# Sixteen-head cross attention: scores with context tokens on partitions, maximum and sum by GpSimd, two heads at a time

## Chip, cores, metric

The program runs on one core of a Trainium2 chip. The core has five engines that run their own queues of instructions and wait for each other by semaphores: TensorE (PE in the profile; its weight loads are PEld), VectorE (DVE), ScalarE (ACT), GpSimd (POOL) and SyncE (SP), which issues the DMAs here. The metric is device time in microseconds (us), the median of several runs. All data is float32.

## What is computed

The reference passes `x` of shape (8 batches, 112 tokens, 512 channels) through four layers, with a context of shape (8, 375, 512). Layer 0 is a plain cross attention, layers 1 and 2 are recurrent token-mixing blocks, and layer 3, which matters here, is a normalization and a cross attention with 16 heads of 128, done twice with different weights, and then a perceptron with one hidden layer:

```python
def _cross_attention(q_in, kv_in, wq, bq, wk, bk, wv, bv, wo, bo, bias_k, bias_v):
    b, q_len, _ = q_in.shape
    t = kv_in.shape[1]
    qh = (q_in @ wq + bq).reshape(b, q_len, H, K)
    kh = (kv_in @ wk + bk).reshape(b, t, H, K)
    vh = (kv_in @ wv + bv).reshape(b, t, H, K)
    kh = jnp.concatenate([kh, jnp.broadcast_to(bias_k, (b, 1, H, K))], axis=1)
    vh = jnp.concatenate([vh, jnp.broadcast_to(bias_v, (b, 1, H, K))], axis=1)
    scale = jnp.sqrt(jnp.asarray(K, q_in.dtype))
    logits = jnp.einsum('bqhk,bthk->bhqt', qh, kh) / scale
    weights = jax.nn.softmax(logits, axis=-1)
    ctx = jnp.einsum('bhqt,bthk->bqhk', weights, vh).reshape(b, q_len, H * K)
    return ctx @ wo + bo
...
x = res + _cross_attention(h, xf_1, ...)
...
x = res + _cross_attention(h, xf_2, ...)
h = _layer_norm(x, ln_mlp_scale, ln_mlp_offset)
h = jax.nn.gelu(h @ w_fc1 + b_fc1, approximate=False) @ w_fc2 + b_fc2
return x + h
```

Each query has 376 scores: 375 context tokens and one learned key, `bias_k`, with the learned value `bias_v`.

## The kernel before

Activations lie with channels on partitions: `x`, `h_in`, `q`, `ctxt` are tiles of 128 partitions with the 896 tokens (8 batches of 112) along the free dimension, one block of 512 channels being four such slices.

**Attention.** `attention(i, ...)` (L1267) runs for i = 1 and 2. Its outer loop goes over 4 groups of 4 heads (`NG`, `HG`), its inner one over 8 batches: 64 batch steps in both attentions. Per group there is a query projection (`queries`, L1357), an output projection (`project7` with `w_o`), and for every second batch the keys of two batches (`key_pieces`, L1277, which runs `chained`, L1206, or, for a few, loads keys made earlier). These products are done by a scheme with seven half-size products in place of eight, for which GpSimd makes sums of weight quarters (`weight_sums`, L1122, lines 1135 to 1138: `ws..`, `wsk`). The values of all batches were computed earlier, beside layers 1 and 2, and lie in memory; each step loads its own (L1398, L1399: tile `v`, one buffer).

**One batch step** (L1393 to L1425) for four heads: GpSimd copies the learned key into column 375 of `kt` (L1396). For each head the score product has the query as the stationary operand (128x112) and the keys as the moving one (376 columns), so that queries lie on partitions: `sc` is 112x376 in PSUM (L1403). `softmax` (L229) takes VectorE's maximum along the row (L232), ScalarE's exponential with the sum accumulated (L235), VectorE's reciprocal (L236) and scaling (L237). TensorE transposes the probabilities in three pieces, tokens to partitions (L1406, `pt`); two copies by VectorE and one by ScalarE bring them to SBUF (L1410, L1412, `pts`). Then 12 products over 125, 125 and 126 tokens give `av` (L1416), and VectorE adds the bias `bv` into `ctxt` (L1423).

**Records.** A float32 product is shown as two matmul records in the trace, a transpose as one.

**PSUM** has eight banks; in layer 3 there are three for `pt`, two for `sc`, one for `av` and two for the projections and keys (`ps`, pool `t3p`).

**Order.** Layer 0 is scheduled by hand; in layer 3 the tile framework's scheduler sets each engine's order from the order in which the code issues instructions, the data they need, and the buffers that are free, so that key products of later batches stand between the steps of the softmax. The same framework puts a load of a GpSimd library into GpSimd's queue wherever an instruction follows whose code the library loaded before does not have. In the program before the change one such load stands in that queue, ahead of the first use.

After the attentions comes the perceptron (`mlp`, L1453). With the last group of the second attention (`ends`) the output projection is done in halves, after batches 4 and 7, and the normalization for the perceptron follows each.

Of the kernel before, what the change touches and what calls it, by code (L numbers as in the profile page):

```python
# [24 lines left out]
ALU = mybir.AluOpType  # L25
# [18 lines left out]
T = S + 1  # L44
CT = S // 3
# [63 lines left out]
def tile_kernel(ctx: ExitStack, tc: tile.TileContext, d: dict, out: bass.AP):  # L109
# [27 lines left out]
    ones_t, mean_h, less_mean_h = (const.tile([P, P], F32, name=f) for f in ("ones_t", "mean_h", "less_mean_h"))  # L137
    pick = const.tile([P, 4, 4 * HB], F32, name="pick")
# [983 lines left out]
    def weight_sums(pool, tag, w, u):  # L1122


        if tag == "kt":
            y = [pool.tile([P, HG, T], F32, tag=tag, name=f"ws{j}{u}", bufs=4) for j in range(2)]
# [140 lines left out]
    def attention(i, ident, h_in, work, kv, ps, ps2, keep, near, mlp_norm):  # L1267
# [9 lines left out]
        def key_pieces(gr, b, w, kts):  # L1277
# [3 lines left out]
            if ("wk", i, gr, b) in shared:  # L1281
                for j in range(2):
                    kts.append(kv.tile([P, HG, T], F32, tag="kt", name=f"k{u}_{j}", bufs=4))
# [13 lines left out]
            kt = [kv.tile([P, HG, T], F32, tag="kt", name=f"k{u}_{j}", bufs=4) for j in range(2)]  # L1297
# [58 lines left out]
        nc.vector.tensor_copy(bv, p)  # L1356
        def queries(gr):  # L1357
# [17 lines left out]

        q, pieces = queries(0)
        for gr in range(NG):
            ends = i == 2 and gr == NG - 1
            w_o = weight(f"{pre}wo{i}", gr)
# [4 lines left out]
            for b in range(B):  # L1384
                u = f"{i}_{gr}_{b}"
                tok = slice(b * L, (b + 1) * L)
                if b % 2 == 0:
                    if gr and not b:
                        w_ks.append(key_weight(gr))
# [6 lines left out]
                nc.gpsimd.tensor_copy(kt[:, :, S], over[:, gr * HG : (gr + 1) * HG])  # L1396
# [3 lines left out]
                pt = [ps2.tile([CT + 1, HG, L], F32, tag="pt", name=f"pt{u}_{t}", bufs=3) for t in range(3)]  # L1400
                for o in range(HG):
                    sc = ps2.tile([L, T], F32, tag="sc", name=f"sc{u}_{o}", bufs=2)
                    nc.tensor.matmul(sc, q[:, o, tok], kt[:, o, :], start=True, stop=True)  # L1403
                    prob = softmax(work, sc, T, f"{u}_{o}")
                    for t, (t0, nt) in enumerate(CHUNKS):
                        nc.tensor.transpose(pt[t][:nt, o, :], prob[:, t0 : t0 + nt], ident[:L, :L])  # L1406
                pts = work.tile([CT + 1, 3, HG, L], F32, tag="pts", name=f"pts{u}", bufs=1)
                for t, (_, nt) in enumerate(CHUNKS):
                    if t == 1:
                        nc.scalar.copy(pts[:nt, t], pt[t][:nt])  # L1410
                    else:
                        nc.vector.tensor_copy(pts[:nt, t], pt[t][:nt])  # L1412
                av = ps2.tile([P, HG, L], F32, tag="av", name=f"av{u}")
                for o in range(HG):
                    for t, (_, nt) in enumerate(CHUNKS):
                        nc.tensor.matmul(  # L1416
                            av[:, o, :],
# [206 lines left out]
```

## Time and profile before

| | |
|---|---|
| median of three runs | 2947.22 us (2944.2 to 2949.86) |
| span of the profiled execution | 2938.3 us |
| layers 0 to 2, values, first keys and queries | 0 to 1472 us |
| first attention's steps | 1472 to 2045 us |
| between the attentions | 2045 to 2127 us |
| second attention's steps | 2127 to 2742 us |
| last output projection and perceptron | 2742 to 2938 us |
| mean granted TensorE clock | 0.996 |

The stretches are read from the timeline, by the starts and ends of score and value products. GpSimd's own costs in the attentions are small: 64 copies of the learned key (223 ns each) and weight sums of 1.3 to 1.5 us each. The profile's rows give a source line, an engine, an operation, the tiles written and read, a count, then the busy time and the mean of one, then the idle time of the engine ahead of it with what ended it.

### The profile page before, as it was taken

To read this page: it belongs to the slowest core of one execution; us is meant where nothing else is said; L and a number is where in the kernel's file an instruction comes from. 1 tells how busy PE (TensorE), PEld (TensorE's weight loads), DVE (VectorE), ACT (ScalarE), POOL (GpSimd) and SP (SyncE) were. 2 spreads that over 40 slices of the span, in tenths; PEclk is the share of its full clock that TensorE was granted. 3 is DMA by queue.
4 is the path that set the end of the run, shared out by engine and by line. 5 is a ranking of instruction groups with operands and counts; after the bars stand their busy time and mean duration, and the time that the engine had idled before them with its cause. 6 is when DMAs were issued, how large, how long until landed. Compare 5 with 4: busy or idle time off the path is not lost.

```text
span 2938.3 us, 29915 instructions
## 1 busy us (share of the span) xinstructions
PE 2848.3 (97%) x10130; PEld 1555.3 (53%) x10130; DVE 1605.4 (55%) x2408; ACT 1020.6 (35%) x2028; POOL 870.8 (30%) x700
## 2 busy tenths in 40 slices
PE   8989999999999999999899999999999999999999
PEld 4734443344444433356465656566565656656544
DVE  1464288845442788652555555545554554545455
ACT  2232456533243565532331313232331323323311
POOL 1432178744331687641412010100302010000030
PEclk9999999999999999999999999999999999999999
DMA  5721498843311989642243334334332433432110
GB/s 208 231 76 39 156 278 258 265 128 110 99 64 62 281 234 298 184 132 90 101 149 126 124 123 129 109 122 140 102 123 100 133 108 122 139 113 80 47 51 25
DMA packets 198743, 400.82 MB, mean 136 GB/s; under 512 B 33224, under 2 KB 119528, under 8 KB 191808
## 3 DMA queue, kind: packets, MB, share of 16 engines
q1 hardware_dynamic: 198592, 398.91, 43.2%
q8 instruction: 81, 1.33, 0.2%
q14 instruction: 70, 0.57, 0.1%
HBM read 321.06 MB, written 77.91 MB: 136 GB/s over the span
## 4 chain that ended last, share of the span: by engine, by line
PE 83%; DVE 9%; ACT 3%; POOL 3%; issue 2%; DMA 1%; DVEq 0%; POOLq 0%; ACTq 0%; SPq 0%
PE ps_vk L1001 13%; PE ps_k1k L1234 10%; PE ps_k5k L1234 7%; PE av L1416 6%; PE sc L1403 5%; PE ps_o L163 3%; PE pt L1406 3%; PE ps_fk L163 2%; PE ps_k1q L1161 2%; PE ps_r L569 2%; PE ps_k L569 2%; PE ps_k5q L1161 2%; PE ps_fr L163 2%; PE ps_v L569 2%; PE ps_k7q L1161 2%
## 5 line engine op out<-in xcount | busy, mean ns | idle before, releaser
L1001 PE MATMUL ps_vk<-wv,cv 128*128 128x512 f32 x1296 | 581.7, 599 | 13.8 <-ACT k L1099 6.1
L1001 PEld LDWEIGHTS ps_vk<-wv,cv 128*128 128x128 f32 x1296 | 242.8, 191 | 337.3 <-issue 285.0
L1027 POOL TENSOR_TENSOR k<-k,k 128x512 f32<-128x512 f32 (+1 forms) x153 | 197.2, 1289 | 323.4 <-ACT k L1026 276.0
L776 DVE TENSOR_TENSOR_SCAN st<-decay,kv 128x904 f32<-128x904 f32 x128 | 260.7, 2037 | 17.5 <-POOL rs L780 4.8
L780 POOL TENSOR_TENSOR rs<-st,r 128x896 f32<-128x896 f32 x128 | 246.8, 1928 | 51.9 <-DVE st L776 46.8
L235 ACT ACTIVATE prob<-sc,top 112x376 f32<-112x376 f32 x256 | 147.2, 575 | 296.3 <-DVE top L232 168.0
L1396 POOL COPY k<-over_k 128x4 f32<-128x4 f32 x64 | 13.8, 223 | 648.6 <-PE sc L1403 576.6
L1403 PE MATMUL sc<-k,q 128*112 128x376 f32 x512 | 201.2, 485 | 1.6 <-ACT prob L235 1.5
L1416 PEld LDWEIGHTS av<-pts,v 125*128 125x128 f32 (+1 forms) x1536 | 183.4, 191 | 31.0 <-DVE pts L1412 15.8
L1416 PE MATMUL av<-pts,v 125*128 125x112 f32 (+1 forms) x1536 | 187.7, 276 | 1.9 <-DVE pts L1412 0.9
L1234 PE MATMUL ps_k1k<-cs,wsk 128*128 128x375 f32 x480 | 177.8, 478 | 4.6 <-ACT u2k L1237 3.1
L772 DVE TENSOR_TENSOR kv<-vp,k 128x904 f32<-128x904 f32 x128 | 141.5, 1105 | 58.2 <-ACT vp L674 52.4
L232 DVE TENSOR_REDUCE top<-sc 112x1 f32<-112x376 f32 x256 | 139.0, 544 | 53.7 <-PE sc L1403 49.0
L1026 ACT COPY k<-ps_vk 128x512 f32<-128x512 f32 (+1 forms) x153 | 89.1, 582 | 177.0 <-PE ps_vk L1001 174.2
L1099 ACT COPY k<-ps_vk 128x512 f32<-128x512 f32 (+1 forms) x153 | 89.0, 582 | 172.3 <-PE ps_vk L1001 164.2
L1406 PEld LDWEIGHTS pt<-ident_l,prob 112*125 112x125 f32 (+1 forms) x768 | 97.3, 175 | 72.2 <-DVE prob L237 44.8
L1406 PE MATMUL pt<-ident_l,prob 112*125 112x112 f32 (+1 forms) x768 | 120.7, 276 | 2.7 <-DVE prob L237 2.5
L1234 PEld LDWEIGHTS ps_k1k<-cs,wsk 128*128 128x128 f32 x480 | 88.7, 188 | 62.8 <-ACT u2k L1237 4.3
L237 DVE TENSOR_SCALAR prob<-prob,total 112x376 f32<-112x376 f32 x256 | 113.4, 443 | 7.7
L1241 DVE TENSOR_TENSOR k<-ps_k5k,u2k 128x375 f32<-128x375 f32 x52 | 28.5, 549 | 162.2 <-PE ps_k5k L1234 161.2
L674 ACT COPY vp<-vj 128x896 f32<-128x896 f32 x124 | 112.8, 910 | 7.3 <-DMA vj<-rows 3.5
L1423 DVE TENSOR_TENSOR ctxt<-av,bv 128x448 f32<-128x448 f32 x64 | 40.0, 625 | 128.9 <-PE av L1416 128.9
(394 smaller groups left out, 4837.0 us busy)
## 6 DMA issues: line engine op xcount, KB each, us to landing
vj<-rows SPq DMA_DIRECT2D x124, 448.0 KB
cv<-blocks SPq DMA_DIRECT2D x181, 251.5 KB
cs<-blocks SPq DMA_DIRECT2D x120, 375.0 KB
wvs<-k SPq DMA_DIRECT2D x128, 256.0 KB
v<-wvs SPq DMA_DIRECT2D x64, 512.0 KB
cx<-in_ctxT SPq DMA_DIRECT2D x38, 750.0 KB
v<-wvs SPq DMA_DIRECT2D x64, 252.0 KB
wvs<-k SPq DMA_DIRECT2D x64, 224.0 KB
```

What stands on the lines that cost most here:

```text
L163: nc.tensor.matmul(p, w[:, k, o * P : (o + 1) * P], rhs(k, h), start=k == 0, stop=k == NC - 1)
L235: nc.scalar.activation(prob, scores, AF.Exp, bias=top, accum_out=total)
L569: nc.tensor.matmul(y, ws[f][:, c, o * P : (o + 1) * P], x_f, start=c == 0, stop=c == NC - 1)
L776: nc.vector.tensor_tensor_scan(flat(st), flat(decay[:, c]), flat(kv), 0.0, ALU.mult, ALU.add)
L780: nc.gpsimd.tensor_mul(by_batch(rs), st[:, :, :L], by_batch(r[:, c, :]))
L1001: nc.tensor.matmul(to, left, right, start=start and n == 0, stop=k == 1, skip_group_check=True)
L1027: nc.gpsimd.tensor_add(y, z, y)
L1161: nc.tensor.matmul(to, lhsT, rhs, start=start and k == 0, stop=k == 1, skip_group_check=not start)
L1234: nc.tensor.matmul(y, lhsT, rhs, start=start and k == 0, stop=k == 1, skip_group_check=True)
L1403: nc.tensor.matmul(sc, q[:, o, tok], kt[:, o, :], start=True, stop=True)
L1406: nc.tensor.transpose(pt[t][:nt, o, :], prob[:, t0 : t0 + nt], ident[:L, :L])
L1416: nc.tensor.matmul(av[:, o, :], v[:nt, t, o * HD : (o + 1) * HD], pts[:nt, t, o, :], start=t == 0, stop=t == 2,)
```

## The change

The score product is turned round: a block of 128 key columns is the stationary operand, the 112 queries of a head the moving one, so that tokens lie on partitions and no transpose is needed. Three blocks start at tokens 0, 125 and 250; each is 128 wide, so that it runs over its own 125 or 126 tokens, and the key tile gets two more columns (`TK`), filled with the learned key. The surplus partitions are taken out by a bias of -1e30 in the exponential (`rests`). The maximum over tokens is then a maximum of three blocks, by VectorE, and one over partitions, by GpSimd's `partition_all_reduce`; the sum likewise, by two GpSimd adds and a second all-reduce. The division is moved behind the value product, with the bias added by ScalarE. All of it is done for two heads at a time, twice in a batch step. PSUM in layer 3 is now four banks for `sc` (two buffers of two banks), one for `av` and three for the projections and keys. The key weight of a group is asked for ahead of the output weight, and four constant tiles of the earlier layers are freed ahead of layer 3.

```diff
+TK = T + 2
...
+    marks = ExitStack()
+    marked = marks.enter_context(tc.tile_pool(name="marks", bufs=1))
+    ones_t, mean_h, less_mean_h = (marked.tile([P, P], F32, name=f) for f in ("ones_t", "mean_h", "less_mean_h"))
+    pick = marked.tile([P, 4, 4 * HB], F32, name="pick")
...
-    ones_t, mean_h, less_mean_h = (const.tile([P, P], F32, name=f) for f in ("ones_t", "mean_h", "less_mean_h"))
-    pick = const.tile([P, 4, 4 * HB], F32, name="pick")
...
-    def softmax(work, scores, n, name):
-
-        top = work.tile([L, 1], F32, tag="top", name=f"top_{name}")
-        nc.vector.tensor_reduce(top, scores, AX.X, ALU.max, negate=True)
-        prob = work.tile([L, n], F32, tag="prob", name=f"prob_{name}")
-        total = work.tile([L, 1], F32, tag="total", name=f"total_{name}")
-        nc.scalar.activation(prob, scores, AF.Exp, bias=top, accum_out=total)
-        nc.vector.reciprocal(total, total)
-        nc.vector.tensor_scalar(prob, prob, total, None, ALU.mult)
-        return prob
...
+        rests = keep.tile([P, 2], F32, tag="rests", name=f"rests{i}")
+        for y, n in enumerate((CT, CT + 1)):
+            nc.vector.tensor_reduce(rests[:, y : y + 1], ident[:, n:], AX.X, ALU.add)
+        nc.vector.tensor_scalar(rests, rests, -1e30, None, ALU.mult)
...
+        def attend(u, gr, heads, q, kt, v, ctxt, tok):
+
+            n = len(heads) * L
+            sc = ps2.tile([P, 4, 256], F32, tag="sc", name=f"sc{u}", bufs=2)
+            for t in range(3):
+                for y, o in enumerate(heads):
+                    nc.tensor.matmul(
+                        sc[:, t, y * L : (y + 1) * L], kt[:, o, t * CT : t * CT + P], q[:, o, tok], start=True, stop=True
+                    )
+            top, tops, each = (work.tile([P, n], F32, tag="top", name=f"{f}{u}", bufs=6) for f in ("top", "tops", "each"))
+            nc.scalar.copy(top, sc[:, 0, :n])
+            for t in (1, 2):
+                nc.vector.tensor_max(top, sc[:, t, :n], top)
+            nc.gpsimd.partition_all_reduce(tops, top, P, ReduceOp.max)
+            pts = work.tile([P, 3, n], F32, tag="pts", name=f"pts{u}", bufs=2)
+            nc.vector.tensor_sub(pts, sc[:, :3, :n], tops.unsqueeze(1).to_broadcast([P, 3, n]))
+            for t, y in ((slice(2), 0), (slice(2, 3), 1)):
+                nc.scalar.activation(pts[:, t], pts[:, t], AF.Exp, bias=rests[:, y : y + 1])
+            nc.gpsimd.tensor_add(tops, pts[:, 0], pts[:, 1])
+            nc.gpsimd.tensor_add(tops, pts[:, 2], tops)
+            nc.gpsimd.partition_all_reduce(each, tops, P, ReduceOp.add)
+            nc.vector.reciprocal(each, each)
+            av = ps2.tile([P, len(heads), L], F32, tag="av", name=f"av{u}")
+            for y, o in enumerate(heads):
+                for t, (_, nt) in enumerate(CHUNKS):
+                    nc.tensor.matmul(
+                        av[:, y],
+                        v[:nt, t, o * HD : (o + 1) * HD],
+                        pts[:nt, t, y * L : (y + 1) * L],
+                        start=t == 0,
+                        stop=t == 2,
+                    )
+            where = ctxt[:, heads[0] : heads[-1] + 1, tok]
+            nc.vector.tensor_mul(where, av, each.rearrange("p (o n) -> p o n", n=L))
+            for y, o in enumerate(heads):
+                nc.scalar.activation(where[:, y], where[:, y], AF.Identity, bias=column(bv, gr * HG + o))
...
+            if gr:
+                w_ks.append(key_weight(gr))
...
-                    if gr and not b:
-                        w_ks.append(key_weight(gr))
...
-                nc.gpsimd.tensor_copy(kt[:, :, S], over[:, gr * HG : (gr + 1) * HG])
+                nc.gpsimd.tensor_copy(
+                    kt[:, :, S:], over[:, gr * HG : (gr + 1) * HG].unsqueeze(2).to_broadcast([P, HG, TK - S])
+                )
                 v = kv.tile([P, 3, C], F32, tag="v", name=f"v{u}", bufs=1)
                 nc.sync.dma_start(v[:, :2], shared["wv", i, gr, b][:, :2])
                 nc.sync.dma_start(v[: CT + 1, 2], shared["wv", i, gr, b][: CT + 1, 2])
-                pt = [ps2.tile([CT + 1, HG, L], F32, tag="pt", name=f"pt{u}_{t}", bufs=3) for t in range(3)]
-                for o in range(HG):
-                    sc = ps2.tile([L, T], F32, tag="sc", name=f"sc{u}_{o}", bufs=2)
-                    nc.tensor.matmul(sc, q[:, o, tok], kt[:, o, :], start=True, stop=True)
-                    prob = softmax(work, sc, T, f"{u}_{o}")
-                    for t, (t0, nt) in enumerate(CHUNKS):
-                        nc.tensor.transpose(pt[t][:nt, o, :], prob[:, t0 : t0 + nt], ident[:L, :L])
-                pts = work.tile([CT + 1, 3, HG, L], F32, tag="pts", name=f"pts{u}", bufs=1)
-                for t, (_, nt) in enumerate(CHUNKS):
-                    if t == 1:
-                        nc.scalar.copy(pts[:nt, t], pt[t][:nt])
-                    else:
-                        nc.vector.tensor_copy(pts[:nt, t], pt[t][:nt])
-                av = ps2.tile([P, HG, L], F32, tag="av", name=f"av{u}")
-                for o in range(HG):
-                    for t, (_, nt) in enumerate(CHUNKS):
-                        nc.tensor.matmul(
-                            av[:, o, :],
-                            v[:nt, t, o * HD : (o + 1) * HD],
-                            pts[:nt, t, o, :],
-                            start=t == 0,
-                            stop=t == 2,
-                        )
-                nc.vector.tensor_add(
-                    ctxt[:, :, tok], av, bv[:, gr * HG : (gr + 1) * HG].unsqueeze(2).to_broadcast([P, HG, L])
-                )
+                for half in range(2):
+                    attend(f"{u}_{half}", gr, range(2 * half, 2 * half + 2), q, kt, v, ctxt, tok)
...
-            tc.tile_pool(name="t3p", bufs=2, space=PSUM) as ps,
+            tc.tile_pool(name="t3p", bufs=3, space=PSUM) as ps,
...
+    marks.close()
     layer3()
```

More of the change, by code (lines that the diff above doesn't have):

```diff
@@ L18 @@
 import concourse.tile as tile
+from concourse.bass_isa import ReduceOp
 from concourse import mybir
@@ L1125, in weight_sums @@
         if tag == "kt":
-            y = [pool.tile([P, HG, T], F32, tag=tag, name=f"ws{j}{u}", bufs=4) for j in range(2)]
+            y = [pool.tile([P, HG, TK], F32, tag=tag, name=f"ws{j}{u}", bufs=4) for j in range(2)]
             y = [t.rearrange("p a b -> p (a b)")[:, : 2 * C].rearrange("p (j k o) -> p j k o", j=2, k=2) for t in y]
@@ L1282, in key_pieces @@
                 for j in range(2):
-                    kts.append(kv.tile([P, HG, T], F32, tag="kt", name=f"k{u}_{j}", bufs=4))
+                    kts.append(kv.tile([P, HG, TK], F32, tag="kt", name=f"k{u}_{j}", bufs=4))
                     for t in range(3):
@@ L1296, in key_pieces @@
             nc.sync.dma_start(b22, d["ctxT"][:, b + 1, 2:])
-            kt = [kv.tile([P, HG, T], F32, tag="kt", name=f"k{u}_{j}", bufs=4) for j in range(2)]
+            kt = [kv.tile([P, HG, TK], F32, tag="kt", name=f"k{u}_{j}", bufs=4) for j in range(2)]
             kts += kt
```

## The prediction

> **What bounds the kernel now.** I read the shares of busy time first, then the chain of work that ended last.
>
> ```profile
> PE 2848.3 (97%) x10130; PEld 1555.3 (53%) x10130; DVE 1605.4 (55%) x2408; ACT 1020.6 (35%) x2028; POOL 870.8 (30%) x700
> ...
> PE 83%; DVE 9%; ACT 3%; POOL 3%; issue 2%; DMA 1%; DVEq 0%; POOLq 0%; ACTq 0%; SPq 0%
> ```
>
> TensorE is busy 97% of the span and is 83% of the chain. The change lies in one stage, so I next cut the span by stage. The columns are the stretch, its length, then busy time (instructions) of PE, PEld, DVE, ACT and POOL, the granted clock, the DMA share and GB/s.
>
> ```profile
> 1614.00:1764.00 150.00, 149.54 (x633) 94.45 (x632) 80.71 (x183) 41.96 (x108) 16.90 (x21) 1.00 0.40 127
> 2580.00:2742.00 162.00, 154.40 (x649) 97.49 (x647) 81.99 (x172) 50.28 (x120) 11.54 (x14) 1.00 0.30 95
> 2742.00:2938.00 196.00, 187.25 (x494) 92.44 (x492) 101.48 (x142) 36.92 (x55) 28.90 (x20) 1.00 0.11 37
> ```
>
> The first row is one group of four heads (eight batches): PE never stops, the clock is full, and GpSimd works 17 us of 150. The scores run from 1472 to 2742 us with one break (2045 to 2127: output projection, normalization and queries between the two attentions), so the attention loops last 573 + 615 = 1188 us, 18.6 us for each of 64 batch steps. The last row is the tail behind them, 196 us. Whatever leaves PE here is a gain, as long as no other engine needs 18.6 us a step.
>
> **What leaves PE.** The timeline of PE (start, length) gives the cadence from start to start:
>
> ```profile
> 1475.68 0.79 PE L1403 MATMUL sc<-k,q 128*112 128x376 f32 x2
> 1476.31 0.78 PE L1406 MATMUL pt<-ident_l,prob 112*125 112x112 f32 x6
> 1476.93 0.80 PE L1403 MATMUL sc<-k,q 128*112 128x376 f32 x2
> ...
> 1503.09 2.83 PE L1416 MATMUL av<-pts,v 125*128 125x112 f32 x24
> 1505.75 0.79 PE L1406 MATMUL pt<-ident_l,prob 112*125 112x112 f32 x6
> ```
>
> A step has 4 score products of 0.63 us (two records each): 2.53 us. Its 12 transposes take 0.62/6 each: 1.25 us. Its 24 value records take 2.66 us. After the change the 4 score products are 12 with 112 moving columns, 24 records of the shape of the value product: 2.66 us by that row. Saved: 2.53 + 1.25 - 2.66 = 1.12 us a step, 72 us in 64 steps. PE would then need (1188 - 72)/128 = 8.7 us for each half step of two heads, the unit in which the new code works.
>
> **What is added, and where.** The softmax of a half step now goes: ScalarE copies one score block, VectorE takes two maxima, GpSimd reduces over partitions, VectorE subtracts, ScalarE takes exponentials, GpSimd adds three blocks (two adds) and reduces again, VectorE takes reciprocals and scales, ScalarE adds the bias. For VectorE and ScalarE I have rows of the like shape; for GpSimd some.
>
> ```profile
> L706 DVE RECIPROCAL gsq<-gsq 128x224 f32<-128x224 f32 x32 | 48.2, 1523 | 24.7 <-ACT gsq L701 24.7
> L1423 DVE TENSOR_TENSOR ctxt<-av,bv 128x448 f32<-128x448 f32 x64 | 40.0, 625 | 128.9 <-PE av L1416 128.9
> L577 ACT ACT_TABLE_LOAD x14 | 18.0, 1283 | 0.2
> L858 POOL TENSOR_TENSOR x<-x,rr 128x448 f32<-128x448 f32 x16 | 18.1, 1128 | 60.1 <-DVE rr L857 60.1
> L445 POOL TENSOR_TENSOR sx<-first,xa 128x4 f32<-128x4 f32 x16 | 9.3, 584 | 0.0
> L971 POOL COPY wv<-wx 128x1024 f32<-128x1024 f32 x1 | 1.2, 1206 | 1.2 <-PE ps_vk L1001 1.2
> L1396 POOL COPY k<-over_k 128x4 f32<-128x4 f32 x64 | 13.8, 223 | 648.6 <-PE sc L1403 576.6
> ```
>
> VectorE: at 1.4 ns a column (625/448) three operations of 224 columns take 0.31 us each and the subtraction of 672 takes 0.94; with the reciprocal, 1.52, that is 3.4 us of 8.7. ScalarE's two copies, exponentials and biases are below that. Neither binds.
>
> GpSimd's queue is the question. The instruction order of the changed program shows 256 all-reduces of 128x224, 256 adds of 128x224, and also 272 instructions that nobody wrote in the diff: loads of a GpSimd library. The all-reduce stands in another library than the two-input add. Of the loads 136 lead to the all-reduce (128 before the second reduction, 8 before the maximum that opens a group) and 136 back (111 before the first add, 25 before weight sums and a key sum). In a half step the queue reads: maximum reduced, load, add, add, load, sum reduced, and then the next half's maximum with no load between. It is serial, since the adds wait for exponentials of this maximum. Behind those adds wait the sum's reduction, the next half's maximum, the `over` column of later keys (which the score product of a later batch waits for) and the weight sums.
>
> Prices. An add: between the rows of 4 and 448 columns, 224 columns take 0.58 + 0.27 = 0.85 us. The all-reduce has no row. Below, a one-input pass: between 223 ns for 4 columns and 1206 for 1024, 0.43 us. Above, folding 128 partitions in halves is seven two-input adds, 5.95 us. It must at least combine and give back, so I take two adds, 1.7 us. The Trainium skill ("GPSIMD Engine Reference", section 3.2 Cross-partition) counts partition-axis reduction among the things GpSimd is for, but its figure for a reduction along partitions of [128, 2048], 247,699 ns, would make 27 us of 224 columns; with that the sum below would be 10.7 ms, an estimate from that page.
>
> A library load has no row either. Below: 1.28 us, what ScalarE needs to load a table. Above, code that comes from memory: these lines show a transfer of 1 MB issued at 0.73 us and first used at 5.94 us, and one of 0.5 MB in the attention stage that the chain waited for.
>
> ```profile
> 0.73 0.40 SPq L127 DMA_DIRECT2D w_L_xattn_w_q_None<-in_L_xattn_w_q  x1
> ...
> 5.94 1.94 PE L327 MATMUL ps_tq<-ident_a,w_L_xattn_w_q_None 128*128 128x128 f32 x8 [5.94 <-DMA w_L_xattn_w_q_None<-in_L_xattn_w_q]
> ...
> 2735.16 3.61 DMA v<-wvs
> ```
>
> That is 5.2 and 3.6 us; two of the longer in a row, 10.4, are my upper end. A load is nearest to such a transfer with an installation behind it: 3.6 + 1.28 = 4.9 or 5.2 + 1.28 = 6.5, and I take the middle, 5.7 us. The same page of the skill (section 2.1, Instruction dispatch) says that the first call to a freshly loaded kernel pays about 6 us, measured 5.95; no trace here shows it, and with that figure the sum would be 272 x 0.25 = 68 us more, an estimate. Against the change stands exactly this rule.
>
> The sum. Gaps between dependent GpSimd instructions show as 0.23 us (a weight sum behind its wait); four of 0.2 make 0.8 us a half step. The first load of a half step covers subtraction (0.94) and exponentials (about 0.65), which would add 1.9 us with their hand-overs if the load were gone. Cycle: 2 x 1.7 + 2 x 5.7 + 2 x 0.85 + 0.8 = 17.3 us against the 8.7 us PE needs. So GpSimd becomes the bound:
> - start of the first reduction: scores at 1472, and their maxima: 1475 us
> - 128 x 17.3 = 2214
> - 16 further loads around weight sums: 91
> - GpSimd's own work that stays in the loops (its busy times between 1472 and 2742 add up to 145, less 26 in the break): 119
> - break between the attentions: 82 + 2 = 84
> - tail: 196 + 2 = 198
>
> Together 4181 us of span against 2938. The median of the runs before, 2947, is 9 above the profiled span, so I predict 4190.
>
> At nothing I cost: the weight of the keys issued before that of the output (1 MB, 5.2 us, behind a GpSimd that is late anyway); the 128x4x3 copy for the former 128x4; the third bank for key products, which shortens waits of PE only; the constants' memory freed ahead of layer 3. Values still come by one buffer: the next load starts when the last half step's products are done and has a cycle of 17 us for its 3.6. If GpSimd kept up, that cover would still be 8.7 us.
>
> **Rivals.** First, GpSimd keeps up, and the change is faster. Its place is the GpSimd queue, its price the PE time saved: 2938 - 72 + 9 = 2875 us. It decides where all-reduce and load together fall below 2.6 us (2 x 2.6 + 2.5 + 0.9 = 8.7). For it speaks GpSimd's idleness today, 133 us of 150; against it, the load's floor of 1.28 and two passes of 0.85 already use 2.1, with the exposed 1.9 us wait on top. Second, loads are cheap (2 us, 1.7 for the reduction): cycle 9.9, 1267 + 32 + 119 + 1757 = 3175, with 9 added 3184; GpSimd binds narrowly. For it: the only load of an engine in this trace, ScalarE's table, takes 1.28 us; against: a library is code that has to be fetched, and the two fetches shown take 3.6 and 5.2. Third, a dear reduction: at 8 us the cycle is 29.9, the span 5794. For it: no GpSimd row here crosses partitions, so nothing measured holds it down; against: seven folds would be enough and cost 5.95. That no library is changed at run time falls under the first and second.
>
> **How the numbers follow.** Forecast 0.80, dear reduction or load 0.10, cheap loads 0.06, GpSimd keeps up 0.04. Low end: load 3.6, reduction 0.85: cycle 11.4, span 3393. High end: load 10.4, reduction 1.7: cycle 26.7, span 5460; a reduction of 5.95 with the middle load gives 5269, within it. Faster by over 0.2% (about what a measurement of this kernel can tell from no change) 0.04, within 0.2% 0.01, slower 0.95.
>
> **What would show it.** PE busy falls from 97% to near 66% (2776 of 4181), idle before value products; the chain passes through POOL; up to 1470 us nothing moves; the DMA queues of kind "instruction" (151 packets, 1.9 MB now) grow by some hundred loads; a group takes near 290 us for 150. If attention lasts about 1116 us with PE full, the load is cheap and I am wrong; if the reductions alone fill the time, the mechanism is the second step, not the load.

## The result, and the profile after

The changed kernel takes 4336.81 us (median of 4 runs, 4324.4 to 4340.21) against 2945.71 us for the kernel before on the same chip: 1.4707 times, 95% interval 1.4681 to 1.4733, or 1391 us more. Its profiled execution has a span of 4332.9 us.

First the page of the changed kernel: the span, the shares of busy time, the granted clock in 40 slices, the two "instruction" DMA queues (packets, MB, share), and the chain of work that ended last.

```profile
span 4332.9 us, 31414 instructions
...
PE 3066.7 (71%) x10386; PEld 1795.0 (41%) x10386; DVE 1650.3 (38%) x2094; ACT 1058.4 (24%) x2092; POOL 1366.5 (32%) x1212
...
PEclk9999999999999976776876875786696597596689
...
q8 instruction: 83, 1.36, 0.1%
q14 instruction: 78, 0.64, 0.1%
...
PE 41%; issue 29%; POOL 12%; DVE 11%; ACT 5%; DMA 2%; SPq 0%; POOLq 0%; DVEq 0%; ACTq 0%
```

PE went from 97% busy to 71%, yet no engine took its place: GpSimd is busy 32%. What fills the chain is "issue", time in which an engine waited for nothing that the profile shows: 29% of the span, some 1257 us, against 2% before. Whose time it is, the waits of GpSimd tell (total, times, longest), and the groups of the page beside them (busy and mean ns of one, then idle time before them):

```profile
POOL each L1394 <- issue: 781.6, 128, 8.6
POOL tops L1392 <- issue: 666.6, 93, 7.9
```

```profile
L1394 POOL PARTITION_ALL_REDUCE each<-tops x128 | 208.4, 1628 | 781.6 <-issue 781.6
...
L1392 POOL TENSOR_TENSOR tops<-pts 128x224 f32<-128x224 f32 x128 | 83.0, 648 | 800.4 <-issue 666.6
...
L1387 POOL PARTITION_ALL_REDUCE tops<-top x128 | 136.3, 1065 | 113.7 <-DVE top L1386 90.0
```

The idle time stands where the instruction order of the changed program has a library load: before each of the 128 sum reductions (781.6 / 128 = 6.1 us) and before 93 of the 111 first adds that have a load (666.6 / 93 = 7.2 us; at the other 18 the trace names another releaser, and all 111 together also have 7.2, from 800.4 us). The maximum's reduction, which follows the sum's with no load between, has no wait at all at 120 of 128. The timeline of the three engines over a little more than one half step, lines of other work left out, shows the cycle (start, length, in brackets the idle time before and its releaser):

```profile
2020.89 1.63 POOL L1394 PARTITION_ALL_REDUCE each<-tops  x1 [5.97 <-issue]
2022.43 1.07 POOL L1387 PARTITION_ALL_REDUCE tops<-top  x1
...
2024.02 0.80 DVE L1389 TENSOR_TENSOR pts<-sc,tops 128x672 f32<-128x672 f32 x1
...
2024.85 0.67 ACT L1391 ACTIVATE pts<-pts,rests 128x448 f32<-128x448 f32 x1 [15.40 <-DVE pts L1389]
...
2025.98 0.47 ACT L1391 ACTIVATE pts<-pts,rests 128x224 f32<-128x224 f32 x1
...
2030.80 0.64 POOL L1392 TENSOR_TENSOR tops<-pts 128x224 f32<-128x224 f32 x1 [7.30 <-issue]
2031.52 0.65 POOL L1393 TENSOR_TENSOR tops<-pts,tops 128x224 f32<-128x224 f32 x1
2037.97 1.63 POOL L1394 PARTITION_ALL_REDUCE each<-tops  x1 [5.80 <-issue]
```

From one sum reduction to the next it is 17.08 us. The exponentials end at 2026.45, and the add starts 4.35 us later: the data is there, the instruction is not. GpSimd computes for 4 of the 17 us and is idle by the page for 13. The whole distance between maxima, 120 of them inside groups, has a median of 17.32 and a mean of 17.80 us. The cut by stage has the columns that the prediction explains. As in the prediction's first row, a group is cut from the end of one group's queries to the end of the next one's, here one of the first attention and one of the second; the last row is the tail behind the last value product:

```profile
2136.00:2445.00 309.00, 171.93 (x642) 120.49 (x641) 84.07 (x138) 44.62 (x111) 74.77 (x79) 0.73 0.18 57
3159.00:3497.00 338.00, 192.28 (x722) 133.44 (x721) 90.14 (x149) 51.27 (x126) 79.61 (x85) 0.75 0.19 60
4131.50:4333.00 201.50, 188.11 (x490) 92.88 (x489) 103.73 (x143) 37.45 (x57) 32.08 (x23) 0.97 0.10 35
```

A group of the first attention is 309 us long (the one ahead of it 321), where it was 150 before, and one of the second 338, where it was 167; GpSimd is busy 75 and 80 of it; the tail is 5 us longer than the 196 before. What the stage table hides is the place between two groups. GpSimd's timeline there:

```profile
2407.34 1.63 POOL L1394 PARTITION_ALL_REDUCE each<-tops  x1 [5.92 <-issue]
2425.15 1.38 POOL L1130 TENSOR_TENSOR ws2q<-w_L_xattn_wq 128x512 f32<-128x512 f32 x1 [16.19 <-PE ps_k7o L1154]
...
2440.41 1.27 POOL L1130 TENSOR_TENSOR ws2o<-w_L_xattn_wo 128x512 f32<-128x512 f32 x1 [9.43 <-PE ps_k7q L1154]
...
2465.21 1.00 POOL L1387 PARTITION_ALL_REDUCE tops<-top  x1 [18.68 <-DVE top L1386]
```

Here the roles change: GpSimd stands for 16, 9 and 19 us, for output projection, queries and the first scores on PE, while no half step is under way. The longest distances between maxima, one for each start of a group inside an attention, are 52.4, 52.5 and 73.2 us in the first attention, 73.6, 73.2 and 73.8 in the second (the two of 52 come one half step after the group's first maximum).

### The profile page after: what moved, and what is told of

Read it like the earlier page. It is cut to its first block, busy times and chain, and to the rows that moved or that the text cites. A ratio compares the mean times of both kernels' runs of the same rounds, so it can differ in the third digit from the quotient of the medians.

```text
span 4332.9 us, 31414 instructions
## 1 busy us (share of the span) xinstructions
PE 3066.7 (71%) x10386; PEld 1795.0 (41%) x10386; DVE 1650.3 (38%) x2094; ACT 1058.4 (24%) x2092; POOL 1366.5 (32%) x1212
## 3 DMA queue, kind: packets, MB, share of 16 engines
q1 hardware_dynamic: 198592, 398.91, 29.4%
## 4 chain that ended last, share of the span: by engine, by line
PE 41%; issue 29%; POOL 12%; DVE 11%; ACT 5%; DMA 2%; SPq 0%; POOLq 0%; DVEq 0%; ACTq 0%
PE ps_vk L994 9%; POOL each L1394 5%; DVE each L1395 4%; PE ps_k1k L1227 2%; PE ps_k5k L1227 2%; PE sc L1380 2%; PE ps_o L167 2%; ACT pts L1391 2%; POOL tops L1393 2%; DVE pts L1389 2%; POOL tops L1392 2%; PE av L1399 2%; PE ps_k7q L1154 1%; PE ps_fk L167 1%; PE ps_k L562 1%
## 5 line engine op out<-in xcount | busy, mean ns | idle before, releaser
L1380 PE MATMUL sc<-q,k 128*128 128x112 f32 x1536 | 316.5, 364 | 852.6 <-DVE pts L1389 852.6
L1380 PEld LDWEIGHTS sc<-q,k 128*128 128x128 f32 x1536 | 284.0, 271 | 904.4 <-issue 791.2
L1395 DVE RECIPROCAL each<-each 128x224 f32<-128x224 f32 x128 | 198.7, 1553 | 1152.3 <-POOL each L1394 1152.3
L1399 PE MATMUL av<-pts,v 125*128 125x112 f32 (+1 forms) x1536 | 330.2, 394 | 217.5 <-ACT pts L1391 216.6
L1391 ACT ACTIVATE pts<-pts,rests 128x448 f32<-128x448 f32 (+1 forms) x256 | 144.3, 567 | 1336.0 <-DVE pts L1389 1336.0
L1394 POOL PARTITION_ALL_REDUCE each<-tops x128 | 208.4, 1628 | 781.6 <-issue 781.6
L1399 PEld LDWEIGHTS av<-pts,v 125*128 125x128 f32 (+1 forms) x1536 | 312.6, 302 | 228.4 <-ACT pts L1391 223.5
L1392 POOL TENSOR_TENSOR tops<-pts 128x224 f32<-128x224 f32 x128 | 83.0, 648 | 800.4 <-issue 666.6
L1386 DVE TENSOR_TENSOR top<-sc,top 128x224 f32<-128x224 f32 x256 | 99.9, 390 | 234.3 <-ACT top L1384 230.2
L1227 PE MATMUL ps_k1k<-cs,wsk 128*128 128x375 f32 x480 | 173.2, 482 | 11.4 <-ACT u2k L1230 8.5
L1387 POOL PARTITION_ALL_REDUCE tops<-top x128 | 136.3, 1065 | 113.7 <-DVE top L1386 90.0
L1409 ACT ACTIVATE ctxt<-ctxt,bv 128x112 f32<-128x112 f32 x256 | 83.4, 373 | 134.7 <-DVE ctxt L1407 134.7
```

Of the source, the lines that this page charges most:

```text
L1227: nc.tensor.matmul(y, lhsT, rhs, start=start and k == 0, stop=k == 1, skip_group_check=True)
L1380: nc.tensor.matmul(sc[:, t, y * L : (y + 1) * L], kt[:, o, t * CT : t * CT + P], q[:, o, tok], start=True, stop=True)
L1391: nc.scalar.activation(pts[:, t], pts[:, t], AF.Exp, bias=rests[:, y : y + 1])
L1392: nc.gpsimd.tensor_add(tops, pts[:, 0], pts[:, 1])
L1394: nc.gpsimd.partition_all_reduce(each, tops, P, ReduceOp.add)
L1395: nc.vector.reciprocal(each, each)
```

## The experiments

A time with a ratio is a median, set against the kernel before on the same chip; a time without one is that of a single execution. "Loads" is the number of GpSimd library loads in the program's instruction order; the changed kernel has 272.

**Two adds on VectorE.** Line numbers are those of the profile.

```diff
-            nc.gpsimd.tensor_add(tops, pts[:, 0], pts[:, 1])
-            nc.gpsimd.tensor_add(tops, pts[:, 2], tops)
+            nc.vector.tensor_add(tops, pts[:, 0], pts[:, 1])
+            nc.vector.tensor_add(tops, pts[:, 2], tops)
```

> The changed kernel with the two adds of a half step on VectorE in place of GpSimd; the weight sums stay on GpSimd, so 88 loads of a library are left of 272. Theory (the loads bind): GpSimd has 88 x 6.6 = 580 us of loads, 128 x 2.7 = 345 us of reductions and 120 us of weight sums in attention loops that need 1116 us of TensorE, so it nearly keeps up: 2880 to 3150 us. Rival (the serial chain of hand-overs through five engines binds, whatever the loads): a half step stays near 17 us and the time within 100 us of 4337.

88 loads are left, and the time is 3507.36 us (3500.9 to 3512.2), ratio 1.1908, 1.1887 to 1.1928. That is 829 us off, far from the theory that only the chain's length counts, but 357 above the upper end of what the load theory asked for. GpSimd's waits in this run:

```profile
POOL tops L1387 <- DVE top L1386: 366.3, 88, 34.0
...
POOL each L1394 <- DVE tops L1393: 266.9, 96, 4.8
POOL each L1394 <- issue: 175.8, 29, 7.5
```

96 sum reductions now wait 2.8 us each for the adds (266.9 / 96), where they had waited 6.1 for nothing; 29 still do that. So 829 / 184 = 4.5 us came back for each load removed, not 6 to 7: a wait for data lay under the load and shows itself when the load goes.

**The adds of two of four heads on VectorE**.

```diff
-            nc.gpsimd.tensor_add(tops, pts[:, 0], pts[:, 1])
-            nc.gpsimd.tensor_add(tops, pts[:, 2], tops)
+            eng = nc.gpsimd if heads[0] else nc.vector
+            eng.tensor_add(tops, pts[:, 0], pts[:, 1])
+            eng.tensor_add(tops, pts[:, 2], tops)
```

> The changed kernel with the two adds on VectorE in the first half of each batch step, on GpSimd in the second: 162 loads in place of 272. Theory of the loads: 110 loads less at 6.1 to 7.2 us take 670 to 790 us away: 3550 to 3670 us. Rival of the chain: no change beyond 50 us, 4290 to 4390.

162 loads, 3873.9 us: between the two expectations. 463 us for 110 loads, 4.2 us each, is close to the net price of the run before (4.5).

**One more change of library in each half step**: a reduction of four columns between the two adds, into a tile that is overwritten next.

```diff
             nc.gpsimd.tensor_add(tops, pts[:, 0], pts[:, 1])
+            nc.gpsimd.partition_all_reduce(each[:, :4], tops[:, :4], P, ReduceOp.add)
             nc.gpsimd.tensor_add(tops, pts[:, 2], tops)
```

> The changed kernel with one more all-reduce, of 4 columns, between the two GpSimd adds of a half step (its result is written over later): 402 loads in place of 272. Theory of the loads: 130 more at 6.1 to 7.2 us, and 128 small reductions of some 0.3 us: 5150 to 5310 us. Rival of the chain: the small reduction alone, 40 to 100 us more: 4380 to 4440.

402 loads, 5234.4 us, as the load theory had it. The added reduction is small work:

```profile
L1393 POOL PARTITION_ALL_REDUCE each<-tops x128 | 62.6, 489 | 392.3 <-issue 368.4
```

0.49 us each, 63 us in all, of 898 us added. The other 835 us fall to 130 more loads, 6.4 us each. Going up, nothing lies beside a load and its whole price shows; going down, part of it was cover. The second add, which here follows the small reduction and has no other engine to wait for, shows the way back to the adds alone:

```profile
POOL tops L1394 <- issue: 799.6, 110, 10.1
```

That is 7.3 us each (799.6 / 110), so the 7.2 before the first add is no disguised wait for the exponentials.

**No two-input arithmetic on GpSimd in this layer.** Besides the two adds, the weight sums (L1128 to L1131) and the key sums (L1232, L1236) go to VectorE.

```diff
-        nc.gpsimd.tensor_add(y[0], a21, a22)
-        nc.gpsimd.tensor_sub(y[1], y[0], a11)
-        nc.gpsimd.tensor_sub(y[2], a11, a21)
-        nc.gpsimd.tensor_sub(y[3], a12, y[1])
+        nc.vector.tensor_add(y[0], a21, a22)
+        nc.vector.tensor_sub(y[1], y[0], a11)
+        nc.vector.tensor_sub(y[2], a11, a21)
+        nc.vector.tensor_sub(y[3], a12, y[1])
...
-                        nc.gpsimd.tensor_add(to, to, add)
+                        nc.vector.tensor_add(to, to, add)
...
-                    (nc.gpsimd if busy else nc.vector).tensor_add(dst(1, 2 + m), dst(1, 2 + m), u3)
+                    nc.vector.tensor_add(dst(1, 2 + m), dst(1, 2 + m), u3)
```

> All two-input arithmetic of layer 3 on VectorE: the adds of the half steps, the weight sums and the sums of the first keys. One load of a library is left in layer 3. Theory of the loads: GpSimd has 345 us of reductions for 1116 us of TensorE's work and TensorE binds again: 2860 to 2900 us, below the kernel before (2946), with the granted clock back at full. Rival of the chain: near 4300. A third way, VectorE overloaded by the weight sums: 2950 to 3050.

One load is left; 3163.94 us (3158.8 to 3169.1), ratio 1.0745, 1.0723 to 1.0768. So 1173 of the 1391 us go with the loads and the move of the adds, but the kernel is still slower than before: the expectation of 2860 to 2900 fails. No reduction over partitions has an "issue" wait in this run's attentions, though GpSimd's copies of the learned key still stand between the reductions. GpSimd's timeline in the middle of a group:

```profile
1862.51 1.61 POOL L1394 PARTITION_ALL_REDUCE each<-tops  x1 [2.67 <-DVE tops L1393]
...
1866.71 0.97 POOL L1387 PARTITION_ALL_REDUCE tops<-top  x1 [2.46 <-DVE top L1386]
1870.35 1.61 POOL L1394 PARTITION_ALL_REDUCE each<-tops  x1 [2.67 <-DVE tops L1393]
```

and VectorE's over the same stretch:

```profile
1864.15 1.55 DVE L1395 RECIPROCAL each<-each 128x224 f32<-128x224 f32 x1 [1.74 <-POOL each L1394]
...
1866.16 0.38 DVE L1386 TENSOR_TENSOR top<-sc,top 128x224 f32<-128x224 f32 x1
1867.72 0.86 DVE L1389 TENSOR_TENSOR pts<-sc,tops 128x672 f32<-128x672 f32 x1 [1.18 <-POOL tops L1387]
...
1869.37 0.39 DVE L1392 TENSOR_TENSOR tops<-pts 128x224 f32<-128x224 f32 x1 [0.34 <-ACT pts L1391]
1869.87 0.39 DVE L1393 TENSOR_TENSOR tops<-pts,tops 128x224 f32<-128x224 f32 x1
```

It is a closed ring of 7.84 us (1862.51 to 1870.35): sum reduced, reciprocal, the next half's maxima (which stand behind the reciprocal in VectorE's queue), maximum reduced, subtraction, exponentials, two adds, sum reduced. No engine is full; each waits for the one before.

The ring alone doesn't set every half step. The products for the keys of two batches spread over four half steps, and in most such sets three distances between maxima are near 7.85 us and the fourth is about 13. One half step at the ring's pace and the fourth one of the same set, from the second attention:

```profile
2470.78:2478.63 7.85, 6.33 (x36) 4.56 (x35) 4.66 (x9) 2.77 (x8) 2.59 (x3) 1.00 0.27 94
2486.62:2499.77 13.15, 11.37 (x53) 8.43 (x54) 5.78 (x10) 3.84 (x10) 2.59 (x3) 0.87 0.64 198
```

PE is busy 6.33 of 7.85 us in the one, and 11.37 of 13.15 in the other, where the key products are that did not fit into the ring's gaps.

**The key sums alone back on GpSimd**: the edit of the last experiment without its last two hunks.

> e5 with the 24 sums of the first keys back on GpSimd: about 9 loads in place of one, order otherwise as e5. Theory of the loads: 8 x 6 to 7 us at most, all in the first group of each attention: 3165 to 3225 us. Rival: as e5, 3160.

8 loads more, 3197.1 us: 33 us, 4.1 us for a load, within the expectation, though this is one execution, and those of the kernel without loads are spread over 10 us. These adds have nothing to do with the softmax.

**Half steps interleaved.** The kernel without loads, with `attend` cut in two: products, maxima and the maximum's reduction of the next half step are issued ahead of subtraction, exponentials, sum and value products of this one.

```diff
             nc.gpsimd.partition_all_reduce(tops, top, P, ReduceOp.max)
+            yield
+            v = values()
...
+                    new = attend(f"{u}_{half}", gr, range(2 * half, 2 * half + 2), q, kt, values, ctxt, tok)
+                    next(new)
+                    if waiting is not None:
+                        next(waiting)
...
+                    waiting = new
```

> e5 (no loads) with the two phases of the half steps interleaved: scores, maxima and the maximum's reduction of the next half step are issued ahead of the exponentials, sum and values of this one. In e5 a half step takes 7.9 us, a closed ring: sum reduced 1.6, reciprocal 1.55 on VectorE, behind which the next maxima stand, maximum reduced 1.0, subtraction 0.86, exponentials 1.04, adds 0.78 and the hand-overs. Theory (this ring, not TensorE, set e5's time): 2870 to 3000 us. Rival (the mere number of operations on VectorE and ScalarE, or the reductions themselves): 3120 to 3180 as e5.

3058.99 us (3051.3 to 3063.4), ratio 1.0381, 1.0356 to 1.0406: 105 us off, in the direction of the ring theory, but above its range. Among PE's waits the value products for the multiply that empties their one PSUM bank come first:

```profile
PE av L1401 <- DVE ctxt L1409: 58.8, 63, 4.2
```

**The same interleaving with the loads left in**: the changed kernel with the last edit, its adds on GpSimd.

> The same interleaving on the changed kernel, with the adds on GpSimd as there: 264 loads in place of 272. Theory of the loads (they fill GpSimd's queue whatever stands between them): 4150 to 4350 us. Rival (the ring of hand-overs is what made the changed kernel slow): below 3700.

264 loads (8 fewer), 4298.49 us, 38 less than the changed kernel. Better order is worth next to nothing while the loads stand in the queue.

**Interleaving with the two adds alone on VectorE**.

> The interleaving on e1 (adds on VectorE, weight sums on GpSimd): 56 loads in place of e1's 88. Theory of the loads and the ring together: below e1 (3507) by more than the 32 loads are worth (210 us), since the ring goes too, and above e6 by 56 x 3 to 7 us = 170 to 390 us: 3050 to 3300. Rival (loads at the groups' ends do not count, since they are hidden): equal to e6.

56 loads, 3236.34 us. Between this and the interleaved kernel without loads lie 177 us, some 3.2 us for each of 55 or so loads, a little under the others.

**Two banks for the value products**, taken from the other products (three to two), in the interleaved kernel.

```diff
-            av = ps2.tile([P, len(heads), L], F32, tag="av", name=f"av{u}")
+            av = ps2.tile([P, len(heads), L], F32, tag="av", name=f"av{u}", bufs=2)
...
-            tc.tile_pool(name="t3p", bufs=3, space=PSUM) as ps,
+            tc.tile_pool(name="t3p", bufs=2, space=PSUM) as ps,
```

> The interleaved half steps without GpSimd's additions (3058.99 us), with two PSUM banks for the value products and two instead of three for the other products. In the interleaved run PE's value products wait 58.8 us in all, 63 waits, for the multiply that empties the one bank. Theory (the one bank holds PE up): at least half of those 58.8 us go, 3000 to 3030 us. Rival (the wait only changes its name: PE then waits for the exponentials or for the third bank that the keys' products lose): 3045 to 3080 us. Either way it stays above the kernel before (2946 us), since 113 us separate them and this wait holds 59.

3076.54 us (3075.4 to 3077.9), ratio 1.0437, 1.0419 to 1.0454: the rival. The wait changes its name, from the multiply to the exponentials, and keeps its size:

```profile
PE av L1401 <- ACT pts L1393: 62.5, 46, 4.3
```

**Value products in the score tile's unused fourth block**, in the interleaved kernel.

```diff
-            av = ps2.tile([P, len(heads), L], F32, tag="av", name=f"av{u}")
+            av = sc[:, 3, : len(heads) * L].rearrange("p (o n) -> p o n", n=L)
```

> The same interleaved kernel, but the value products of a half step go into the unused fourth block of that half step's own score tile, so that they have two places without taking a bank from the keys' products; in return a score tile is held until the context is multiplied. Theory (the one bank holds PE up): 3000 to 3030 us, as far down as the run with two banks or further. Rival (the score tiles, held longer, now hold up the next half step's scores): 3070 to 3150 us, with waits of PE's score products for the multiply or the bias in place of the present ones.

3122.91 us (3122.47 to 3125.71), ratio 1.0596, 1.0575 to 1.0617: again the rival. PE's waits (the second row is that of the value products, which write into `sc` here):

```profile
PE sc L1380 <- DVE ctxt L1409: 85.1, 89, 5.1
PE sc L1401 <- ACT pts L1393: 59.9, 51, 4.5
```

**No reductions over partitions**, in the interleaved kernel: each partition's own maximum and own sum are used, and the surplus partitions' bias is -1.

```diff
-            nc.gpsimd.partition_all_reduce(tops, top, P, ReduceOp.max)
...
-            nc.vector.tensor_sub(pts, sc[:, :3, :n], tops.unsqueeze(1).to_broadcast([P, 3, n]))
+            nc.vector.tensor_sub(pts, sc[:, :3, :n], top.unsqueeze(1).to_broadcast([P, 3, n]))
...
-            nc.gpsimd.partition_all_reduce(each, tops, P, ReduceOp.add)
-            nc.vector.reciprocal(each, each)
+            nc.vector.reciprocal(each, tops)
```

> The interleaved kernel (3058.99 us) with both reductions over partitions left out: the scores are lowered by each partition's own maximum, the sum is each partition's own, and the bias of surplus partitions is -1 instead of -1e30. GpSimd then has no part in the softmax. It shows what the turned products alone are worth. Theory (the 72 us that the prediction took from PE are there, and the reductions' round trips eat them): 2870 to 2920 us, below the kernel before. Rival (the turned products and half steps themselves cost PE its cover: one bank, values and keys late): 2950 to 3040 us.

2895.1 us (2893.38 to 2900.37), ratio 0.9831, 0.9817 to 0.9846: the theory. The turned products, with the half steps interleaved, are worth 51 us, as long as nobody has to wait for GpSimd. Its page:

```profile
PE 2787.8 (96%) x10386; PEld 1581.1 (55%) x10386; DVE 1771.3 (61%) x2494; ACT 1067.3 (37%) x2092; POOL 685.1 (24%) x556
```

VectorE is as busy here (1771 us) as in the interleaved kernel at 3059 us (1773), so VectorE's load, with the adds on it, isn't what costs the time there. It is a measure of a part, not a version to use: it computes another softmax.

**The ring with one member less**: the kernel without loads, not interleaved, without its reciprocal; the context is multiplied by the sum.

```diff
             nc.gpsimd.partition_all_reduce(each, tops, P, ReduceOp.add)
-            nc.vector.reciprocal(each, each)
```

> The kernel with all additions on VectorE (3163.94 us, no interleaving) with the reciprocal left out: the context is multiplied by the sum instead. It takes 1.55 us out of VectorE's queue, in which the next half step's maxima stand behind it. Theory (a closed ring of some 7.9 us from one sum's reduction to the next holds PE up, and the reciprocal is one member): 128 x 1.55 = 198 us of ring go, of which PE's own need of some 8.7 us for a half step lets at most the remaining idle time through: 3010 to 3090 us. Rival (the reciprocal lies beside other work): 3140 to 3170 us.

3022.4 us (3019.86 to 3024.77), ratio 1.0258, 1.0241 to 1.0275: 142 us off, the theory. The median distance between maxima inside a group goes from 7.85 to 6.16 us, by 1.7 where the reciprocal takes 1.55: it does stand on the ring. No work left PE; a member of the ring between its products got shorter. Not all of it reaches the end, since more of the key products are left for the fourth half step:

```profile
2376.41:2382.56 6.15, 4.59 (x31) 3.66 (x30) 2.63 (x6) 2.29 (x7) 2.72 (x4) 1.00 0.07 12
2387.94:2404.17 16.23, 14.93 (x70) 10.07 (x69) 5.32 (x11) 5.22 (x13) 2.80 (x4) 1.00 0.59 184
```

That one grows from 13.15 to 16.23 us, with PE busy 14.93 of it, so that the mean distance falls by 1.06 us, from 8.89 to 7.83.

None of the versions with the whole computation is faster than the kernel before: the best, interleaved and without loads, is 3.8% behind it.

## Why the prediction held

Predicted were 4190 us, slower, by library loads that make GpSimd's queue the bound; measured were 4337. Point by point:

**The mechanism: shown.** More loads make the kernel slower by 6.4 us each, fewer make it faster by about 4 (3.2 to 4.5), and it doesn't matter which adds cause them. All but one of them gone, with the adds moved, takes 1173 of the 1391 us back. It is the change of library, not the adds, that costs: an add of a half step takes 0.65 us, and adding nothing but small reductions between the adds cost 898 us.

**The cycle: 17.3 us predicted, 17.32 the median between maxima.** That the sum is right to the last digit is luck: it is off in its parts, which cancel. A load: 5.7 predicted; the gap before the sum's reduction is 6.1 and the gap before the first add 7.2, 13.3 us together for 11.4. A reduction: 1.7 predicted; 1.63 for the sum and 1.07 for the maximum, 2.7 for 3.4. An add: 0.85 predicted; 0.65, 1.3 for 1.7. The gaps of 0.8 that the prediction set apart are within the loads' gaps. The prediction let the first load cover subtraction and exponentials; the timeline shows that they end 4.35 us before the add starts, so that step holds. That the load came out near the middle of two transfers says nothing of where its code comes from: no run shows it.

The Trainium skill ("GPSIMD Engine Reference", section 2.1, Instruction dispatch) gives 5.95 us for the first call of a freshly loaded kernel, "with no visible profile instruction". The gap of 6.1 us agrees, the one of 7.2 is longer by a fifth, and the trace adds that it is paid again at every change: before all 128 sum reductions and all 111 first adds that have a load. The figure of section 3.2 is for a `tensor_reduce`; scaled to 224 columns, which made 27 us, it doesn't carry over to this all-reduce, which takes 1.07 and 1.63 us.

**The sum's mis-sized term: the work around the loops.** The span is 4332.9 us and the sum was 4181, 152 short, of which 145 lie between the first and the last maximum of each attention; the rest is 5 at the start, 7 in the break between the attentions, and 6 less at the end. For 126 distances between maxima (63 in each attention) the prediction has 126 x 17.3 + 91 (16 further loads) + 119 (GpSimd's own work) = 2390 us; the trace has 1251.85 + 1283.16 = 2535, or 145 more. The 120 distances inside groups sum to 2136 us, 60 above 120 x 17.3, which is half of the 119. The six at a group's start sum to 399 us, 295 above 6 x 17.3, where the sum left room for 150, if the 16 loads and the other half of GpSimd's work are put there. What was overlooked is not GpSimd's work but its idleness: the timeline between groups shows it standing for output projection, queries and first scores. The prediction let this PE work run beside GpSimd's cycles, and it comes in line with them. The kernel without reductions, whose softmax doesn't use GpSimd, takes 321 us for the same six places (between its reciprocals): this is time in which PE works and GpSimd isn't needed.

**The unchanged parts.** Start: first maximum reduced at 1480 us for 1475. Tail, from the end of the last value product: 201 us for 198.

**The 72 us of PE.** In the kernel without reductions PE is busy 2788 us for 2848, 60 less, and 51 us reach the end (2895 for 2946).

**The first rival's limit was wrong.** It said that GpSimd keeps up where reduction and load together fall below 2.6 us, because two of them, adds and hand-overs then fit into PE's 8.7 us. Without loads the reductions take 1.07 and 1.63, far below it, and the kernel takes 3164, not 2875. (The sum there, 2 x 2.6 + 2.5 + 0.9, is 8.6, and GpSimd's work in the break is 24 us by the trace, not 26; neither moves the forecast by more than 2 us.) Two things failed in it. The 8.7 us is a mean over the whole attention, and about a quarter of that is the work between groups: in the kernel without reductions the 120 distances inside groups, measured between reciprocals, average 6.85 us. And the test compared a queue's load with PE's, where the length of the ring decides: without loads it holds most half steps at 7.85 us, the key products that it keeps from PE lengthen about every fourth, and the distance inside a group averages 8.89 us. (8.89 - 6.85) x 120 = 245 us, nearly all of the 261 us between the two kernels' spans (3159.9 and 2898.5). With the reciprocal out it is 7.83, and (7.83 - 6.85) x 120 = 118 of 124 us. So the ring is shown by taking a member out, and by its disappearance with the reductions, while 1.06 of the reciprocal's 1.55 us come off the average.

**The signs.** A group of some 290 us for 150: 309 and 321, as the sign left little for the start of a group (the prediction's own sum, 2214 + 91 + 119 over 8 groups, gives 303). Nothing moves before 1470: PE is busy 1409 us there, before 1403. The chain through POOL: only 12%, and "issue" 29%; the prediction looked for the load under the engine's name, and the profile books it as idle time. Hundreds more packets on the "instruction" queues: wrong, 161 for 151, and 165 with 402 loads (84 and 81). Whoever had judged by that sign would have dismissed the right mechanism. PE at 66%: 71%, because PE itself got slower. Right after a wait of 14 us its timeline shows four products of the same shape at twice and then 1.3 times their later time:

```profile
2412.22 3.35 PE L1154 MATMUL ps_k6o<-t_c,ws1o 128*128 128x448 f32 x4 [14.09 <-DVE t_c L1137]
2415.37 2.17 PE L1154 MATMUL ps_k7o<-ctxt,ws2o 128*128 128x448 f32 x4
2417.37 1.67 PE L1154 MATMUL ps_k5o<-t_c,ws0o 128*128 128x448 f32 x4
```

The granted clock over the same stretch goes up with it, 0.50, then 0.95, then 1.00:

```profile
2412.00:2416.00 4.00, 3.77 (x5) 1.85 (x6) 1.16 (x4) 0.00 (x0) 0.00 (x0) 0.50 0.00 0
2416.00:2420.00 4.00, 4.00 (x11) 2.03 (x10) 3.28 (x6) 0.00 (x0) 0.00 (x0) 0.95 0.00 0
2420.00:2430.00 10.00, 10.00 (x27) 4.78 (x26) 6.25 (x10) 0.00 (x0) 4.43 (x4) 1.00 0.08 13
```

Over a group it is 0.73 to 0.75, in the tail 0.97. The Trainium skill ("TensorE: Matmul & The Clock Gate", Part 1) says that PE is throttled to half its clock after an idle stretch of some 3.4 us and freed by as long a busy one, and 3.35 for 1.67 us at a granted 0.50 agrees. With as many products PE is busy 3067 us here and 2788 in the kernel without reductions, but inside a group the slower PE costs little: 120 of the 128 maxima's reductions start with no wait, so GpSimd's queue sets the cycle.

**What stays open.** Between the interleaved kernel and the one without reductions lie 164 us. PE's waits change their names from run to run (multiply, exponentials, key sums) when banks are moved, so a longer pipeline than one half step might be needed; that wasn't tried. Where the load's time goes inside GpSimd, and why the way back to the adds takes 1.1 us longer, no run shows. Of the runs with one execution (162, 402, 264, 9 and 56 loads) the prices of a load are rough to some tenths of a us.

## What to carry to other kernels

Before work is given to an idle engine, count not only how long its instructions take but what changes between them: two kinds of instruction that need different code, taken in turns, cost some 13 us a pair of changes here, with the engine shown as idle. Compare the ring of hand-overs of one step, not the busy shares, with what the bound engine needs in that stage, and take that need from the stage itself rather than from a mean that includes the work between the loops. A cost that is removed gives back only what it stood above the next wait: 6.4 us for a load that was added, about 4 for one taken away.

## What the runs showed of the hardware

- A load of a GpSimd library leaves no busy time and next to no DMA packets (161 on the "instruction" queues for 151 before, with 272 loads for one; 198592 on the other queue both times). In 93 of 111 cases ahead of an add, and in all 128 ahead of a sum's reduction, it is found as "issue" idle time before the first instruction that needs the other library.
- It is not symmetric: 6.1 us on average towards the all-reduce (5.76 to 8.6), 7.2 towards the adds (6.7 to 7.9 where the idle time is "issue").
- By the profile, whose spans on GpSimd are rough, an all-reduce over 128 partitions takes 1.63 us for a sum of 224 columns and 1.07 for a maximum, 0.49 for a sum of 4 columns.
- A reciprocal of 128x224 takes 1.55 us on VectorE, four times an add of the same shape (0.39), and taking it out of a ring of 7.85 us took 142 us off the kernel, as the next maxima stand behind it in the queue.
